# The first block of a time-mix and FFN kernel: order of the k and r chunks, three of r's chunks in three float32r passes, and weight splits moved to the second block

## The chip, the core and the metric

The kernel runs on one core of a Trainium2 chip. The time is device microseconds of one execution. Engines are named as in the profile: PE (TensorE, matrix products), DVE (VectorE), ACT (ScalarE), POOL (GpSimd) and SP (SyncE, which issues most DMAs).

## The reference

For x of shape (4, 1024, 512) in fp32, with xn the layernorm of x:

```python
xx = concat([xn[:, 1:2], xn[:, :-1]], axis=1) - xn
k  = (xn + xx * time_mix_k) @ Wk.T        # 704 channels
r  = (xn + xx * time_mix_r) @ Wr.T
state_t = state_{t-1} * exp(-exp(time_decay)) + relu(k_t)
mix = layernorm((state * r) @ Wv.T) * ln_gamma + ln_beta
D   = gelu(fp16(xn) @ W0.T + bias0).astype(fp16)   # 2048 hidden units
ffn = (D @ W1.T + bias1).astype(fp16)
out = x + mix + ffn
```

## The kernel before, in words

The 4 x 1024 tokens are worked in eight **blocks** of 512 tokens. In every block the FFN is a loop over 16 **chunks** of 128 hidden units: `up` (L860) makes the accumulator pd of a chunk from 8 matmuls, four with the high halves of w0 and four with fp16 low halves; the gelu (L874) and a cast (L877) on ACT make d from it; `down` (L886) adds the chunk to four accumulators pe with 8 matmuls. `up` runs two chunks ahead of `down`. The time mix of the same block is woven into these chunks by hand: `piece(n, ...)` gives FFN chunk n a group of matmuls, `put(n, ...)` gives it jobs for the other engines, and `behind_w1[n]` a job after all these. Each engine works through its instructions in the order in which the code records them.

**k and r.** The 704 channels are five chunks of 128 and a half chunk. A matrix product with a full chunk takes one of two forms:

- In block 0, plain fp32: `raw_k` (L634), `raw_r` (L648), 4 matmuls with the weights as loaded; `raw_halves` (L658) makes the half chunks of k and r in 32 matmuls of 64 rows.
- In later blocks, `three_pass` (L687): weights and inputs are split into float32r terms; pa takes 8 matmuls (L693), pb takes 4 (L444); ACT copies pa out with a scale (`a`, L705) and DVE adds pb (`y`, L706). `half_pass` (L716, L722) does the half chunks.

k goes through a relu and the scan over tokens (L585); r is multiplied into the state (`gated`, L602).

**Splits.** `split_kr` (L290) makes the three float32r terms of a weight chunk: on DVE `u` (L278), `d` (L287) and term 2 (L298), on ACT two copies (L296, L297); the terms are stored to DRAM, and `load_kr` (L327) fetches them in later blocks. `split_x` does the like for inputs (L278, L338, L340, and L336 on ACT). `split_wv` (L309 on) splits the output weights; its half chunk, `split_wv(5)`, takes two operations on DVE (vu, vd) and four copies of 64 rows on ACT (L324, L325). `split` (L198 to L200) makes the high half of w0 or w1 on ACT and the low half on DVE; `load_w1` calls it in block 0 at the end of a chunk's jobs for the w1 of two chunks on, and `down` begins with the low half there.

**The next block's inputs.** During a block its successor's x is loaded, its statistics taken (L357), normalized (L361) and transposed in 16 `turn`s (L383), and mixed.

**Accumulators.** pd, pk, pr, pa, pb, ph, po, oa and ob share four PSUM banks of the pool `ps_mm` (`bank`). A bank can be written again when its reader is done: ACT for pd (gelu) and pa (`a`), DVE for pb (`y`). In blocks from 1 on the gelu of chunk n + 2 is recorded at the end of chunk n's jobs when n is odd, and after the next chunk's first steps when n is even.

**Before the FFN** block 0 makes k0, k1, k2 (L444, in pieces as the inputs come) and r0, r1, r2, and splits the first groups of w0 and w1.

Of the kernel before, what the change touches and what calls it, by code (L numbers as in the profile page):

```python
# [22 lines left out]
def time_mix_and_gelu_ffn(  # L23
# [40 lines left out]
    Q = 32  # L64
    QS = 62
    RAW_OUT = 1
    WV_FIRST = {0: 12, 1: 13, 2: 15, 3: 15, 5: 15}
    S = 4096.0
    WS = 4096.0
    MASK = -4096  # L70
# [57 lines left out]
    def load_raw(kind, h):  # L128
        w = part(f"w{'kr'[kind]}_{h}", F32)
        raw_w[kind, h] = w.rearrange("p (c k) -> p c k", c=NC)  # L130
        src = sources[kind].rearrange("(c p) k -> p c k", p=P)
        nc.sync.dma_start(raw_w[kind, h], src[:, :, h * P : (h + 1) * P])
# [32 lines left out]
    with tc.manual_schedule(engines={nc.sync.engine, nc.scalar.engine}):  # L165
        x_now = load_x(
            0,
            "x",
            (
                lambda: None,  # L170
                load_mix_rows,
                lambda: [load_raw(0, h) for h in range(FIRST)],
                load_late_rows,
            ),
        )
        for h in range(FIRST):
            load_raw(1, h)
    raw_half = part("raw_half", F32).rearrange("p (two c k) -> p two c k", two=2, c=NC)
    gamma_sb = const.tile([P, C], F32, name="gamma_sb")
    beta_sb = const.tile([P, C], F32, name="beta_sb")  # L180
# [27 lines left out]
    def load_w0(g, c, **home):  # L208
        w0_raw[c, g] = raw = part(f"w0raw_{g}_{c}", F32, **home)
        nc.sync.dma_start(raw, w0T[c * P : (c + 1) * P, g * TB : (g + 1) * TB])  # L210
# [21 lines left out]
        for n in range(NN)  # L232
    ]
    w1_raw = {}
    stores, late_stores = [], []

    def store_weights():
        while stores:
# [34 lines left out]
    half_w = [part(f"half_w_{kind}", tag="half", bufs=2) for kind in range(2)]  # L273
    half_w = [w.rearrange("p (c two k) -> p c two k", c=NC, two=2) for w in half_w]

    def truncated(raw, name, home=None):
        u = (home or temp)(name)
        nc.vector.tensor_scalar(u.bitcast(I32), raw.bitcast(I32), MASK, None, ALU.bitwise_and)  # L278
        return u

    begun = {}

    def begin_kr(kind, h, home):
        raw = raw_w[kind, h].rearrange("p c k -> p (c k)")
        u = truncated(raw, f"wu_{kind}_{h}", home)
        d = home(f"wd_{kind}_{h}")
        nc.vector.tensor_sub(d, raw, u)  # L287
        return u, d

    def split_kr(block, kind, h, **home):  # L290
        made.add((kind, h))
        name = f"{kind}_{h}"
        u, d = begun.pop((kind, h), None) or begin_kr(kind, h, temp)
        home = home or dict(tag="kr", bufs=6)
        terms = [part(f"wt_{name}_{p}", **home) for p in range(3)]
        nc.scalar.copy(terms[0], u)  # L296
        nc.scalar.activation(terms[1], d, AF.Copy, scale=S)  # L297
        nc.vector.scalar_tensor_tensor(terms[2], d, -S, u, ALU.mult, ALU.add)  # L298
        later = late_stores if (kind, h) == (1, NF - 1) else stores
        for p in range(3):  # L300
            later.append((kr_dram[kind, h][p].bitcast(F32), terms[p].bitcast(F32)))
        return [t.rearrange("p (c k) -> p c k", c=NC) for t in terms]

    def split_half():
# [123 lines left out]

    def split_xk(i, c):
        xks[i, c] = yield from split_x(xks[i, c], f"k_{i}_{c}")  # L430

    def split_xr(i, c):
        xrs[i, c] = yield from split_x(xrs[i, c], f"r_{i}_{c}")
# [251 lines left out]
        return after  # L685

    def three_pass(j, kind, h):  # L687
        xs = xks if kind == 0 else xrs
        w = ks.pop((j, kind, h))
        pa, pb = bank(f"pa_{j}_{kind}_{h}"), bank(f"pb_{j}_{kind}_{h}")  # L690
        for c in range(NC):
            for p in range(2):
                nc.tensor.matmul(  # L693
                    pa,
                    w[p][:, c, :],
                    xs[j, c][p],
                    start=(c == 0 and p == 0),
                    stop=(c == NC - 1 and p == 1),
                )
        for c in range(NC):  # L700
            product(pb, w[2], xs[j, c][2], c)

        def after():
            a, y = temp(f"a_{j}_{kind}_{h}"), temp(f"y_{j}_{kind}_{h}")
            nc.scalar.activation(a, pa, AF.Copy, scale=1.0 + 1.0 / S)  # L705
            nc.vector.scalar_tensor_tensor(y, pb, -1.0 / S, a, ALU.mult, ALU.add)  # L706
            if kind == 0:
                nc.scalar.activation(y, y, AF.Relu)  # L708
                yield
                scanned(j, h, P, state_tile(j, h), y)  # L710
            else:
                yield from gated(j, h, y)

        return after
# [194 lines left out]
    with tc.manual_schedule(engines={nc.sync.engine}):  # L909
        for c in range(NC):  # L910
            load_w0(0, c)
        for n in range(AHEAD + 2):
            load_w1_raw(n)
        for h in range(FIRST, NF):
            load_raw(0, h)
            load_raw(1, h)
        for kind, src in enumerate(sources):
            nc.sync.dma_start(
                raw_half[:, kind], src.rearrange("(c p) k -> p c k", p=P)[:, :, H0:]
            )  # L920
        for c in range(NC):
            load_w0(1, c)
        x_next = load_x(1, "x")
        for c in range(NC):
            load_w0(2, c)
# [4 lines left out]

    engines = {e.engine for e in (nc.tensor, nc.vector, nc.scalar, nc.sync)}
    with tc.manual_schedule(engines=engines):
        for kind in range(2):
            begun[kind, 0] = begin_kr(kind, 0, lambda name: part(name, F32))
        first_x16(0)
        for h in range(FIRST):
            finished(raw_k(0, h, pks[h])())
        for c in range(1, NC):
            first_x16(c)
        xf = ffn_input(0)  # L940
        finished(raw_r(0, 0)())
        several(split_w0, (0, 0), (0, 1))
        finished(raw_r(0, 1)())
        several(split_w0, (0, 2), (0, 3))
        w1s = [load_w1(0, n) for n in range(AHEAD)]
        gated_last = raw_r(0, 2)
        several(split_w0, (1, 0), (1, 1))
        several(split_kr, (1, 0, 0), (1, 1, 0))
        finished(gated_last())
        waiting = []  # L950
        for n in range(AHEAD):
            products, gelu = up(0, n)
            several(products, *[(p,) for p in HIGH_FIRST])
            waiting.append((gelu(), w1s[n]))
            split_w0(1, 2 + n)
        store_weights()
# [4 lines left out]
    with tc.manual_schedule(engines=engines):  # L961
        for i in range(len(blocks)):
# [3 lines left out]
            pieces, bg, early = defaultdict(list), defaultdict(list), defaultdict(list)  # L966
            behind_w1 = defaultdict(list)

            def put(n, fn, *args):
                bg[n].append(lambda: fn(*args))  # L970

            def fetch_kr(block, kind, h):
                if (kind, h) not in made:
# [25 lines left out]

            if i == 0:  # L1000
                state["x"] = x_next
                piece(1, raw_k, i, 3)
                piece(3, raw_r, i, 3)
                piece(5, raw_k, i, 4)
                piece(7, raw_r, i, 4)
                piece(9, raw_halves, i)
                for c in range(NC):
                    put(2 + c - (c == 0), split_w0, 2, c)
                    put(c // 2, load_w0, 3, c)
                    put(5 + c, split_w0, 3, c)  # L1010
                put(1, stats, *range(NS))
                put(3, lambda: norm_apply(j, state["x"]))
                for n, *which in (
                    (0, 1, 2), (1, 0, 1), (1, 1, 3), (3, 0, 2), (5, 0, 3), (7, 0, 4), (7, 1, 1)
                ):
                    if which in ([1, 2], [1, 3]):
                        behind_w1[n].append(lambda w=which: split_kr(1, *w, **OWN))
                    else:
                        put(n, split_kr, 1, *which)
                put(4, turn, 0, 1)  # L1020
                put(5, turn, 1, 5)
                put(7, turn, 5, 10)
                put(8, turn, 10, 11)
                put(9, turn, 11, 16)
                put(9, load_late_constants)
                put(12, split_half)
                for g in range(NN // G):
# [3 lines left out]
            else:  # L1031
                order = [(0, h) for h in range(NF)] + [(1, h) for h in range(NF)]
                halves_ahead_of = (3 if i == LAST else NF, NF)
                for k, (kind, h) in enumerate(order):
                    for half in range(2):
                        if k == halves_ahead_of[half]:
                            piece(half_at[half], half_pass, i, half)
                    piece(full_at[k], three_pass, i, kind, h)
                    if (kind, h) not in made:
                        put(1, fetch_kr, i, kind, h)  # L1040
                    elif k > 1:
                        put(full_at[k - 2], fetch_kr, i, kind, h)
                xr_at = {1: (2, 3, 4, 5), LAST: (1, 2, 2, 3)}.get(i, (2, 2, 3, 3))
# [15 lines left out]
            if j <= LAST:  # L1059
                for c in range(NC):  # L1060
                    put((10, 10, 11, 12)[c], x16, j, c)
                for c, n in enumerate(mix_at):
                    early[n].append((j, c))
                    put(n, mixed, j, c)
                    put(n + (n == 10), split_xk, j, c)
                for h, n in {0: WV_FIRST, 1: {NF - 1: 2}}.get(i, {}).items():
                    put(n, split_wv, h)
                put(13, fetch_kr, j, 0, 0)
                put(14, fetch_kr, j, 0, 1)

            pe = [ps_e.tile([P, C], F32, tag="pe", name=f"pe_{i}_{s}") for s in range(NS)]
            for n in range(NN):
# [68 lines left out]
                    behind_works.append(lambda gelu=gelu, w1=w1: (gelu(), w1))  # L1141
                elif paired:
                    waiting.append((gelu(), w1))
                if (i, n) == (1, 6):
                    stores.extend(late_stores)
                store_weights()
            if not tail:
                e16s = [rounded(i, s, pe[s]) for s in range(NS)]
# [64 lines left out]
```

## Time and profile before

| what | us |
| --- | --- |
| median of 3 runs | 853.61 (853.30 to 853.65) |
| profiled execution | 853.32 |
| its span | 851.5 |
| PE busy | 847.1 |
| DVE busy | 678.1 |
| ACT busy | 434.0 |
| PE in block 0 from 40.80 to 130.40 | 89.51 of 89.60 |
| PE in block 1, 130.40 to 233.70 | 103.30 of 103.30 |

The page of the profile first gives the busy time of each engine, then the span in 40 slices with busy tenths in each. The chain of waits, further down, is followed back from the last instruction to what released each step: a row is its start in us, its duration, engine, tile and source line. A timeline lists one engine's instructions in order: start, duration, engine, line, operation, the tile written and the tiles read, their shapes; in brackets stands the idle time ahead of it and what ended it.

The raw chunks ahead of the FFN and in it, the FFN's pd and pe and the three-pass chunks all lie on PE, one after the other; the jobs for DVE and ACT lie beside them.

### The profile page before, as it was taken

Reading aid. Unit: us, or ns where it says so; the run is one execution under the profiler, and the core shown is the slowest. Engines: PE = TensorE matmul, PEld = TensorE weight load, DVE = VectorE, ACT = ScalarE, POOL = GpSimd, SP = SyncE. Lnnn points to the kernel's source line nnn. Section 1 sums busy time; section 2 is a strip of 40 time slices with the busy share of each in tenths; the row PEclk is TensorE's granted clock in tenths of the full one; section 3 lists DMA queues with packets and bytes.
Section 4 is the critical chain, followed back from the end, with each engine's and each line's share of the span. In section 5 each row is a group of like instructions: output and inputs, shape, how many; then the busy total and the mean of one; then the engine's idle time right before and its main releaser. Section 6 shows DMA issues by size and latency. Waiting matters only on the chain.

```text
span 851.5 us, 11300 instructions
## 1 busy us (share of the span) xinstructions
PE 847.1 (99%) x3756; PEld 592.4 (70%) x3756; DVE 678.1 (80%) x1114; ACT 434.0 (51%) x740; POOL 77.5 (9%) x145
## 2 busy tenths in 40 slices
PE   9999999999999999999999999999999999999998
PEld 8555546776766777766767767767767667776776
DVE  7689898898868978689786888779796897876446
ACT  5866764556444572544634456344653545534422
POOL 1100000000121002000021001100011200200002
PEclk9999999999999999999999999999999999999999
DMA  9976976753485635846458455494455755467513
GB/s 291 342 250 239 297 212 224 229 189 124 149 283 174 210 121 159 288 154 194 161 168 283 146 167 180 160 304 146 154 184 171 267 169 184 125 222 248 168 55 112
DMA packets 121766, 168.30 MB, mean 198 GB/s; under 512 B 21583, under 2 KB 57836, under 8 KB 121708
## 3 DMA queue, kind: packets, MB, share of 16 engines
q1 hardware_dynamic: 121260, 166.91, 60.7%
q8 instruction: 30, 0.49, 0.2%
q10 hardware_dynamic: 448, 0.66, 0.2%
q14 instruction: 28, 0.23, 0.1%
HBM read 142.88 MB, written 24.64 MB: 197 GB/s over the span
## 4 chain that ended last, share of the span: by engine, by line
PE 95%; DVE 3%; ACT 1%; issue 0%; DMA 0%; ACTq 0%
PE pd L860 26%; PE pe L886 26%; PE pa L693 15%; PE oa L790 7%; PE pb L444 7%; PE ob L798 4%; PE ph L722 3%; PE po L749 2%; PE pr L444 2%; PE ob L800 1%; PE pk L444 1%; PE pkr L667 0%; DVE stx L357 0%; DVE wd L287 0%; DMA x<-in_L_attn_x 0%
## 5 line engine op out<-in xcount | busy, mean ns | idle before, releaser
L886 PE MATMUL pe<-w,d 128*128 128x512 f32 (+1 forms) x1008 | 262.0, 388 | 0.1
L860 PE MATMUL pd<-xf,w0h 128*128 128x512 f32 x512 | 151.7, 418 | 0.0
L860 PE MATMUL pd<-x,w0l 128*128 128x512 f16 x512 | 132.2, 381 | 0.0
L874 ACT ACTIVATE d<-pd,late_sb 128x512 f16<-128x512 f32 x128 | 87.1, 681 | 81.5 <-PE pe L886 51.8
L860 PEld LDWEIGHTS pd<-xf,w0h 128*128 128x128 f32 x512 | 96.1, 188 | 29.0 <-issue 4.3
L886 PEld LDWEIGHTS pe<-w,d 128*128 128x128 f32 x504 | 94.7, 188 | 22.1
L706 DVE SCALAR_TENSOR_TENSOR y<-pb,a 128x512 f32<-128x512 f32 x70 | 48.2, 689 | 65.6 <-PE pb L444 55.3
L886 PEld LDWEIGHTS <-d 128*128 128x128 f16 x524 | 50.6, 98 | 60.4 <-issue 1.2
L860 PEld LDWEIGHTS <-w0l 128*128 128x128 f16 x512 | 44.1, 98 | 62.4 <-issue 17.4
L877 ACT CAST d<-d 128x512 fp32r<-128x512 f16 x128 | 79.4, 620 | 10.3 <-PE pe L886 6.3
L383 DVE STREAM_TRANSPOSE xnT<-x 32x512 f32<-32x512 f32 x112 | 78.7, 702 | 2.2
L705 ACT ACTIVATE a<-pa 128x512 f32<-128x512 f32 x70 | 41.8, 597 | 72.5 <-PE pa L693 72.3
L351 POOL TENSOR_SCALAR ry<-mvy 128x1 f32<-128x1 f32 x32 | 18.8, 589 | 421.2 <-DVE mvy L358 421.2
L693 PE MATMUL pa<-hk,kr 128*128 128x512 f32 x140 | 54.5, 389 | 0.0
L693 PE MATMUL pa<-lk,kr 128*128 128x512 f32 x140 | 54.5, 389 | 0.0
L790 PE MATMUL oa<-wv,hg 128*128 128x512 f32 x140 | 54.5, 389 | 0.0
L790 PE MATMUL oa<-wv,lg 128*128 128x512 f32 x140 | 54.5, 389 | 0.0
L693 PE MATMUL pa<-hr,kr 128*128 128x512 f32 x136 | 52.9, 389 | 0.0
L693 PE MATMUL pa<-lr,kr 128*128 128x512 f32 x136 | 52.9, 389 | 0.0
L708 ACT ACTIVATE y<-y 128x512 f32<-128x512 f32 x35 | 22.1, 631 | 52.7 <-DVE y L706 52.7
L805 DVE SCALAR_TENSOR_TENSOR oy<-ob,oa 128x512 f32<-128x512 f32 x28 | 19.3, 689 | 26.2 <-PE ob L800 26.2
L336 ACT CAST hg<-ug 128x512 fp32r<-128x512 f32 x35 | 21.7, 620 | 34.6 <-DVE ug L278 34.5
(167 smaller groups left out, 1387.1 us busy)
## 6 DMA issues: line engine op xcount, KB each, us to landing
kr<-krd SPq DMA_DIRECT2D x207, 256.0 KB, 4.3
w<-w1d SPq DMA_DIRECT2D x112, 256.0 KB, 2.7
w<-w1d SPq DMA_DIRECT2D x112, 128.0 KB, 2.7
w0l<-w0d SPq DMA_DIRECT2D x108, 128.0 KB, 3.5
xres<-in_L_attn_x SPq DMA_DIRECT2D x32, 256.0 KB, 4.7
x<-in_L_attn_x SPq DMA_DIRECT2D x31, 256.0 KB, 4.9
krd<-wt SPq DMA_DIRECT2D x30, 256.0 KB, 2.3
out<-xres SPq DMA_DIRECT2D x28, 256.0 KB, 3.5
```

The lines of the kernel that those rows point to most:

```text
L383: nc.vector.transpose(dst[i * Q : (i + 1) * Q, :, :, j, :], src[j * Q : (j + 1) * Q, :, :, i, :],)
L444: return nc.tensor.matmul(dst, w[:, c, :], src, start=(c == 0), stop=(c == NC - 1))
L693: nc.tensor.matmul(pa, w[p][:, c, :], xs[j, c][p], start=(c == 0 and p == 0), stop=(c == NC - 1 and p == 1),)
L705: nc.scalar.activation(a, pa, AF.Copy, scale=1.0 + 1.0 / S)
L706: nc.vector.scalar_tensor_tensor(y, pb, -1.0 / S, a, ALU.mult, ALU.add)
L722: nc.tensor.matmul(pa, w[:, c].rearrange("p two k -> p (two k)"), xs[j, c][p], start=(c == 0 and p == 0), stop=(c == NC - 1 and p == 1),)
L790: nc.tensor.matmul(pa, gs[i, h][p][:, cols], wv[h][p], start=(h == 0 and p == 0), stop=(h == NF - 1 and p == 1),)
L798: nc.tensor.matmul(pb, gs[i, h][2][:, cols], wv[h][2], start=(h == 0), stop=False)
L860: nc.tensor.matmul(pd, weights(c, p), src[c][p], start=(c == 0 and p == order[0]), stop=(c == NC - 1 and p == order[1]),)
L874: nc.scalar.activation(d16, pd, AF.Gelu, bias=b0_sb[:, n : n + 1], scale=1.0 / WS)
L877: nc.scalar.copy(d, d16)
L886: nc.tensor.matmul((sums or pe)[s], d[p][:, s * P : (s + 1) * P], w1[p][:, cols], start=(n == first and p == order[0]), stop=(n == end(s) ...
```

## The change

Block 0 and block 1 are reordered; blocks 2 to 7 keep their code.

- Ahead of the FFN, all five full chunks of k (raw) and r0, instead of k0 to k2 and r0 to r2. The begun splits there (r's and k's chunk 0) and `split_kr(1, 0, 0)`, `split_kr(1, 1, 0)` are taken out.
- In block 0's FFN: the half chunks at chunk 1 (were at 9), raw r4 at chunk 3, and r1, r2, r3 by `three_pass` at chunks 5, 7, 9 (raw k3, r3, k4, r4 stood at 1, 3, 5, 7). The r inputs are split for this (`split_first_xr`, three at chunk 0, one at chunk 1) and r's weight chunks 1 to 3 at chunks 3, 5, 7.
- k's chunks 0, 1 and 2 are split at chunks 10, 11 and behind w1 at 5. The splits of k's chunks 3 and 4 and of r's chunks 0 and 4 move to block 1, at its FFN chunks 1, 2, 4, 6 (before, one split of a chunk stood there, r's chunk 4, at chunk 1). These four are used in block 1 as they are made.
- `split_wv(5)` moves from block 0's chunk 15 to block 1's chunk 3, `split_wv(4)` in block 1 from chunk 2 to 8.
- The turns at chunks 7, 8, 9 become 5 to 11, 11 to 12, 12 to 16. The raw weights are loaded in another order. The late stores of r's chunk 4 go with the others.

```diff
-    WV_FIRST = {0: 12, 1: 13, 2: 15, 3: 15, 5: 15}
+    WV_FIRST = {0: 12, 1: 13, 2: 15, 3: 15}
...
-        for h in range(FIRST):
-            load_raw(1, h)
+        for which in ((0, 3), (0, 4), (1, 0)):
+            load_raw(*which)
...
+    first_xr = {}
+
+    def split_first_xr(c):
+        first_xr[0, c] = yield from split_x(xrs[0, c], f"r_0_{c}")
...
     def three_pass(j, kind, h):
-        xs = xks if kind == 0 else xrs
+        xs = xks if kind == 0 else xrs if j > 0 else first_xr
...
-        for h in range(FIRST, NF):
-            load_raw(0, h)
-            load_raw(1, h)
         for kind, src in enumerate(sources):
             nc.sync.dma_start(
                 raw_half[:, kind], src.rearrange("(c p) k -> p c k", p=P)[:, :, H0:]
             )
+        for h in (4, 1):
+            load_raw(1, h)
         for c in range(NC):
             load_w0(1, c)
+        for h in (2, 3):
+            load_raw(1, h)
...
-        for kind in range(2):
-            begun[kind, 0] = begin_kr(kind, 0, lambda name: part(name, F32))
...
-        finished(raw_r(0, 0)())
+        finished(raw_k(0, 3)())
         several(split_w0, (0, 0), (0, 1))
-        finished(raw_r(0, 1)())
+        scanned_last = raw_k(0, 4)
         several(split_w0, (0, 2), (0, 3))
+        finished(scanned_last())
         w1s = [load_w1(0, n) for n in range(AHEAD)]
-        gated_last = raw_r(0, 2)
+        gated_last = raw_r(0, 0)
         several(split_w0, (1, 0), (1, 1))
-        several(split_kr, (1, 0, 0), (1, 1, 0))
         finished(gated_last())
...
-                piece(1, raw_k, i, 3)
-                piece(3, raw_r, i, 3)
-                piece(5, raw_k, i, 4)
-                piece(7, raw_r, i, 4)
-                piece(9, raw_halves, i)
+                piece(1, raw_halves, i)
+                piece(3, raw_r, i, NF - 1)
+                for h in range(1, NF - 1):
+                    piece(2 * h + 3, three_pass, i, 1, h)
...
-                for n, *which in (
-                    (0, 1, 2), (1, 0, 1), (1, 1, 3), (3, 0, 2), (5, 0, 3), (7, 0, 4), (7, 1, 1)
-                ):
-                    if which in ([1, 2], [1, 3]):
-                        behind_w1[n].append(lambda w=which: split_kr(1, *w, **OWN))
-                    else:
-                        put(n, split_kr, 1, *which)
+                for c in range(NC):
+                    put(c // 3, split_first_xr, c)
+                for h in range(1, NF - 1):
+                    put(2 * h + 1, first_kr, h)
+                put(10, split_kr, 1, 0, 0, **OWN)
+                put(11, split_kr, 1, 0, 1, **OWN)
+                behind_w1[5].append(lambda: split_kr(1, 0, 2, **OWN))
                 put(4, turn, 0, 1)
                 put(5, turn, 1, 5)
-                put(7, turn, 5, 10)
-                put(8, turn, 10, 11)
-                put(9, turn, 11, 16)
+                put(7, turn, 5, 11)
+                put(8, turn, 11, 12)
+                put(9, turn, 12, 16)
...
                     if (kind, h) not in made:
-                        put(1, fetch_kr, i, kind, h)
+                        put({(0, 3): 1, (0, 4): 2, (1, 0): 4, (1, 4): 6}[kind, h], fetch_kr, i, kind, h)
...
-                for h, n in {0: WV_FIRST, 1: {NF - 1: 2}}.get(i, {}).items():
+                for h, n in {0: WV_FIRST, 1: {NF: 3, NF - 1: 8}}.get(i, {}).items():
                     put(n, split_wv, h)
...
-                if (i, n) == (1, 6):
-                    stores.extend(late_stores)
```

More of the change, by code (lines that the diff above doesn't have):

```diff
@@ L234, in time_mix_and_gelu_ffn @@
     w1_raw = {}
-    stores, late_stores = [], []
+    stores = []
     def store_weights():
@@ L274, in time_mix_and_gelu_ffn, with truncated, begin_kr @@
     half_w = [w.rearrange("p (c two k) -> p c two k", c=NC, two=2) for w in half_w]
-    def truncated(raw, name, home=None):
-        u = (home or temp)(name)
+    def truncated(raw, name):
+        u = temp(name)
         nc.vector.tensor_scalar(u.bitcast(I32), raw.bitcast(I32), MASK, None, ALU.bitwise_and)
         return u
-    begun = {}
-    def begin_kr(kind, h, home):
+    def begin_kr(kind, h):
         raw = raw_w[kind, h].rearrange("p c k -> p (c k)")
-        u = truncated(raw, f"wu_{kind}_{h}", home)
-        d = home(f"wd_{kind}_{h}")
+        u = truncated(raw, f"wu_{kind}_{h}")
+        d = temp(f"wd_{kind}_{h}")
         nc.vector.tensor_sub(d, raw, u)
@@ L292, in split_kr @@
         name = f"{kind}_{h}"
-        u, d = begun.pop((kind, h), None) or begin_kr(kind, h, temp)
+        u, d = begin_kr(kind, h)
         home = home or dict(tag="kr", bufs=6)
@@ L298, in split_kr @@
         nc.vector.scalar_tensor_tensor(terms[2], d, -S, u, ALU.mult, ALU.add)
-        later = late_stores if (kind, h) == (1, NF - 1) else stores
         for p in range(3):
-            later.append((kr_dram[kind, h][p].bitcast(F32), terms[p].bitcast(F32)))
+            stores.append((kr_dram[kind, h][p].bitcast(F32), terms[p].bitcast(F32)))
         return [t.rearrange("p (c k) -> p c k", c=NC) for t in terms]
@@ L967, in time_mix_and_gelu_ffn, with put, first_kr @@
             behind_w1 = defaultdict(list)
-            def put(n, fn, *args):
-                bg[n].append(lambda: fn(*args))
+            def put(n, fn, *args, **home):
+                bg[n].append(lambda: fn(*args, **home) if home else fn(*args))
+            def first_kr(h):
+                ks[0, 1, h] = split_kr(0, 1, h)
             def fetch_kr(block, kind, h):
```

## The prediction

> **What bounds the kernel now.** I read the page from the top: the busy shares, the row of 40 slices, the chain of waits, then the timelines of VectorE (DVE), ScalarE (ACT) and TensorE (PE) where the change edits them. The page:
>
> ```profile
> PE 847.1 (99%) x3756; PEld 592.4 (70%) x3756; DVE 678.1 (80%) x1114; ACT 434.0 (51%) x740; POOL 77.5 (9%) x145
> PE   9999999999999999999999999999999999999998
> DVE  7689898898868978689786888779796897876446
> ```
>
> PE is the bound: 847.1 of 851.5 us, at the full granted clock in every slice, so PE work removed is gained and each PE wait added is paid in full at the end. But DVE is at 0.8 to 0.9 in block 0 and block 1 (the first nine or ten slices), where the change adds to it. The windows by block say it closer: DVE was busy 77.90 of the 89.60 us from 40.80 to 130.40 (block 0) and 90.01 of the 103.30 us of block 1, against 83.48 in block 2. The chain of waits over the first 135 us:
>
> ```profile
> 54.92 0.69 DVE w0l L200
> 55.61 1.83 DVE x L361 x4
> ...
> 59.73 0.70 DVE w L200
> ...
> 60.47 1.94 PE pe L886 x8
> 62.41 3.44 PE pk L444 x8
> ...
> 73.01 3.44 PE pr L444 x8
> ...
> 83.75 3.59 PE pkr L667 x32
> ...
> 130.51 1.81 PE pa L693 x8
> 132.33 0.91 PE pb L444 x4
> ```
>
> Up to 60.4 the split of w1 by DVE (L200) ends the wait and PE follows; from 60.47 PE runs alone. A raw chunk (two rows above, 8 records) is 3.44 us, a chunk in three passes 1.81 + 0.91 = 2.72 (last two rows). How thin the margin is stands in DVE's timeline:
>
> ```profile
> 77.47 3.56 DVE L383 STREAM_TRANSPOSE xnT<-x 32x512 f32<-32x512 f32 x5
> 81.06 0.69 DVE L200 SCALAR_TENSOR_TENSOR w<-w1raw,w 128x512 f16<-128x512 f32 x1
> ```
>
> This is the low half of w1 for chunk 9; it ends at 81.75, and PE's down matmuls of chunk 9, which begin with that half, start at 81.80. PE came with no margin: whatever delays DVE here delays PE.
>
> **PE's own work.** r1, r2, r3 go from 3.44 to 2.72: 3 x 0.72 = **2.16 us less**. Raw k3, k4, r0, r4, the halves (3.59) and all else only change places. Ahead of the FFN k3, k4 stand where r1, r2 stood, same shapes and same count; I take the first FFN matmuls where they were.
>
> [...]
>
> **Block 0's DVE.** New: four splits of x_r (12 DVE operations, 7.2 us at the 0.6 of a neighbouring split's pitch), y's of three chunks (0.69 each). Gone from block 0: the splits of k's chunks 3 and 4, r's 0 and 4 (1.8 each: 0.45+0.72+0.61), and wv_5 from chunk 15. I laid the changed kernel's list of DVE instructions out with these durations. w1's low half starts at (before / after): w1_5 59.73 / 58.78, w1_6 62.72 / 61.78, w1_7 69.74 / 68.83, w1_8 72.07 / 74.14, w1_9 81.06 / 82.63. From w1_7 to w1_9 are 11.32 us before, 13.80 after: the split of k's chunk 2 behind w1 at chunk 5 (+1.8), one split fewer at chunk 7 (-1.8), a sixth turn (+0.72), and waits for ACT copies (0.56, 0.42, 1.08 against 0.41: +1.65); y and g stand for the scan. The sum is 2.4; the layout's 2.48 is used.
>
> PE after, from pe of chunk 5 at about 60.5: r1 in place of k4, r2 in place of r4, so that it wants pe of chunk 9 at 80.26 (81.80 less 2 x 0.72; its first pe, with no wait before it, is 0.16 shorter, and starts 0.03 later). The low half of w1_9 is ready at 83.37. **Stall 3.1 us.** Then r3 (2.72) stands for the halves (3.59 plus the slower pd after it), 1.0 less, so chunk 10's pe comes at 89.75 against 89.18. The later low halves come 1 to 4 us later than before but at least 1.3 us ahead of PE. So block 0 eats its whole gain: block 1 begins **0.55 late** (bounds: -0.9, were w1_9 on time for all but 1.6 us, to +1.2).
>
> **Block 1, three waits.** Before, PE had none here. An accumulator bank (four, L444 and L860 share them) is free again when ACT has read it. In the changed kernel's instruction list pa of k's chunk 4 waits for d16_5 (gelu of pd_5), pa of r's chunk 1 for d16_9, pa of r's chunk 2 for the copy `a` of r's chunk 1. Before, ACT had them early:
>
> ```profile
> 152.36 0.62 ACT L336 CAST hr<-ur 128x512 fp32r<-128x512 f32 x1 [0.44 <-DVE ur L278]
> 152.89 0.68 ACT L874 ACTIVATE d<-pd,late_sb 128x512 f16<-128x512 f32 x1
> ...
> 175.15 0.62 ACT L620 CAST gh<-gl 64x512 fp32r<-64x512 f32 x1 [0.82 <-DVE gl L619]
> 175.80 0.69 ACT L874 ACTIVATE d<-pd,late_sb 128x512 f16<-128x512 f32 x1
> ...
> 180.79 0.60 ACT L705 ACTIVATE a<-pa 128x512 f32<-128x512 f32 x1 [0.59 <-PE pa L693]
> ```
>
> and PE began those pa at 155.63, 178.94 and 186.97.
>
> 1. The four copies of wv_5 (L324, L325) now stand on ACT between hr and d16_5 at chunk 3. They wait for vu_5, which DVE reaches only after the pair of stats (before 153.70 to 155.39, after to 155.44) plus 0.42: 155.86. Four copies at 0.66 (before, at chunk 15: 125.56 to 128.26, 2.70): to 158.53. d16_5 to 159.20. pa, wanted at 155.63 + 0.55 = 156.2, starts at 159.25: **+3.05**. If the copies were hidden, 0; nothing hides them, since ACT's rows start in the order of its list.
> 2. Behind that, `a` of k's chunk 3 comes at 160.3, y at 160.4, and DVE has the splits of r's chunk 0 (chunk 4) and r's chunk 4 (chunk 6), 3.6 us, that it had not; it runs without idle time. y of the half pass starts at 179.63 (before 171.82), gl follows as before, the copy gh at 182.95, then d16_9, 183.60 to 184.29. pa is wanted at 178.94 + 3.6 = 182.55 and starts at 184.3: **+1.7**.
> 3. wv_4's split (DVE 1.8) with its ACT copy at 192.9 stands ahead of the copy `a` of r's chunk 1 (193.4 to 194.0), which before ran at 180.79. pa of r's chunk 2 is wanted at 186.97 + 5.4 = 192.35, starts 194.0: **+1.7**.
>
> After that splits (wv_4 was at chunk 2) are behind it, PE's shift gives DVE time, and the margins are 0.5 to 3 us; the three kr chunks that are split here are not loaded (9 DMAs of 256 KB fewer; the kr issues take 4.3 us to land, and no wait in block 1 was for one). Blocks 2 to 7 have the same work in the same order. Of the moved DMAs, SP's list has nine issues fewer; raw loads go earlier than the halves, and the first to be needed at chunk 1 are the halves, 40 us after the start. I find none that lands late and put 0 on it (bounds -0.2 to +1).
>
> **Sum.** +0.55 + 3.05 + 1.7 + 1.7 = **+7.0**; with rounding in the layout, 7.06. The profiled execution took 853.32 us (span 851.5), the median of the three runs is 853.61, so the sum goes on 853.32: **860.4 us**.
>
> **Rivals.**
> - *The gain stays.* DVE keeps w1_9 before 80.3 and ACT d16_5 before 156.2, and the 2.16 us of PE time is all that counts: 853.32 - 2.16 = **851.2**. For it: PE alone is on the chain from 60.47. Against: the zero margin at 81.8 with 2.5 us more of DVE ahead of it. It is decided by those two times. Chance 0.09.
> - *Block 0's stall alone.* vu_5 is early enough or pa does not wait for d16_5: +0.55, **853.9**, within 0.2% (1.7 us, about what a measurement of this kernel can tell from no change). For it: the times in block 1 are worked out over 100 us of DVE. Chance 0.09.
> - *Some of the three waits.* The first remains and the next two, each less than 2 us and hung on DVE's lag, are absorbed: +3.6, **856.9**. For it: their two prices are differences of long sums. Chance 0.20.
> - *More lag.* DVE does not catch up before the out stage, and a fourth wait of the same size (1.7 to 3) follows: **863**. Chance 0.10.
> - *The forecast*, 858 to 862.5: chance 0.52.
>
> Faster by over 0.2% is only the first rival: 0.09. Same: the second: 0.09. Slower: 0.82. The range takes the forecast, the third and part of the last: **855.3 to 863**.
>
> **What would show it.** In the changed profile: pr rows in float32r of 1.81 + 0.91 at chunks 5, 7, 9 (right on PE's 2.16); a DVE w1 low half on the chain near 83, before pe of chunk 9 (right on block 0); block 1's pa of k's chunk 4 waiting 3 us for ACT's d16, with four wv copies ahead of it; two later waits near 183 and 193; block 2 as long as before. I am wrong if PE shows no idle time at 80 to 84, or if the idle time in block 1 lies behind a DMA.

## The result, and the profile after

The changed kernel takes 861.66 us (median of 4 runs, 861.63 to 862.13), the kernel before 853.63 (4 runs, 853.30 to 853.98): a ratio of 1.0095, 95% interval 1.0078 to 1.0113. It is 8.0 us slower. The profiled execution took 861.63, its span is 859.8 us.

The page of the changed kernel, the rows that answer to those shown of before, and PE's granted clock:

```profile
PE 847.3 (99%) x3768; PEld 594.9 (69%) x3768; DVE 686.3 (80%) x1129; ACT 436.9 (51%) x747; POOL 79.8 (9%) x145
...
PE   9998999899999999999999999999999999999998
...
DVE  6788898799877988789886897868796897876446
...
PEclk9999999999999999999999999999999999999999
```

PE was busy for as long as before (847.3 against 847.1), though it has less to do; the span is 8.3 longer, so PE now waits. Two slices of PE, the fourth and the eighth, stand at 8. Its waits, added up by what ended them (line, releaser, us in all, times, longest):

```profile
PE pa L695 <- ACT d L876: 3.6, 2, 2.2
PE pe L888 <- DVE w L200: 3.0, 1, 3.0
PE pa L695 <- ACT a L707: 1.4, 1, 1.4
```

Before, none of these three groups existed. In PE's timeline the four waits lie one after the other (the idle time stands in brackets):

```profile
83.55 3.45 PE L888 MATMUL pe<-w,d 128*128 128x512 f16 x8 [2.95 <-DVE w L200]
...
160.04 0.50 PE L695 MATMUL pa<-hk,wt 128*128 128x512 f32 x1 [2.24 <-ACT d L876]
...
185.12 0.50 PE L695 MATMUL pa<-hr,kr 128*128 128x512 f32 x1 [1.35 <-ACT d L876]
...
194.83 0.50 PE L695 MATMUL pa<-hr,kr 128*128 128x512 f32 x1 [1.38 <-ACT a L707]
```

The first row has something that a wait does not explain: eight pe matmuls took 3.45 us, against 1.94 before. The windows of the changed kernel around it tell why (stretch, its length, busy times of PE, PEld, DVE, ACT, POOL; then the granted clock, DMA share, GB/s):

```profile
78.00:80.60 2.60, 2.60 (x12) 1.49 (x11) 2.54 (x4) 2.57 (x6) 0.00 (x0) 1.00 0.79 295
80.60:83.50 2.90, 0.00 (x1) 0.00 (x0) 2.83 (x6) 2.28 (x5) 0.00 (x0) 0.97 0.26 98
83.50:85.00 1.50, 1.45 (x5) 0.61 (x4) 1.47 (x3) 0.00 (x0) 0.00 (x0) 0.50 0.26 87
85.00:86.00 1.00, 1.00 (x3) 0.78 (x3) 0.97 (x2) 0.00 (x0) 0.00 (x0) 0.50 0.96 178
86.00:87.00 1.00, 1.00 (x4) 0.79 (x3) 0.94 (x3) 0.00 (x0) 0.00 (x0) 0.63 0.88 336
87.00:88.00 1.00, 1.00 (x7) 0.80 (x6) 0.99 (x2) 0.63 (x1) 0.00 (x0) 1.00 0.26 91
```

PE stood still from 80.6 to 83.5, and at about 83.3 its clock fell to half, until about 86.7. What it did until then took about twice as long.

How far PE is behind the kernel before, at the points which the prediction named (start of the first matmul, from the timelines; forecast as summed there):

| PE starts | before | after | later by | forecast |
| --- | --- | --- | --- | --- |
| first pd | 29.61 | 29.70 | 0.09 | 0 |
| pe of chunk 9 | 81.80 | 83.55 | 1.75 | 1.57 |
| pe of chunk 10 | 89.18 | 91.35 | 2.17 | 0.57 |
| block 1, pa of k's chunk 0 | 130.35 | 132.52 | 2.17 | 0.55 |
| block 1, pa of k's chunk 4 | 155.47 | 160.04 | 4.57 | 3.6 |
| block 1, pa of r's chunk 1 | 178.78 | 185.12 | 6.34 | 5.3 |
| block 1, pa of r's chunk 2 | 186.80 | 194.83 | 8.03 | 7.0 |
| profiled execution | 853.32 | 861.63 | 8.31 | 7.06 |

From block 2 on nothing is added that matters (8.03 to 8.31).

### The profile page after: what moved, and what is told of

Read it like the earlier page. It is cut to its first block, busy times and chain, and to the rows that moved or that the text cites. A ratio compares the mean times of both kernels' runs of the same rounds, so it can differ in the third digit from the quotient of the medians.

```text
span 859.8 us, 11343 instructions
## 1 busy us (share of the span) xinstructions
PE 847.3 (99%) x3768; PEld 594.9 (69%) x3768; DVE 686.3 (80%) x1129; ACT 436.9 (51%) x747; POOL 79.8 (9%) x145
## 4 chain that ended last, share of the span: by engine, by line
PE 77%; DVE 3%; ACT 0%; issue 0%; DVEq 0%
PE pd L862 21%; PE pe L888 21%; PE pa L695 13%; PE oa L792 7%; PE pb L446 7%; PE ob L800 4%; PE ph L724 3%; PE ob L802 1%; DVE xnT L380 1%; DVE xres L841 0%; DVE x L358 0%; DVE e L835 0%; DVE y L708 0%; DVE mr L337 0%; DVE lr L335 0%
## 5 line engine op out<-in xcount | busy, mean ns | idle before, releaser
L708 DVE SCALAR_TENSOR_TENSOR y<-pb,a 128x512 f32<-128x512 f32 x73 | 50.2, 688 | 69.6 <-PE pb L446 54.9
L707 ACT ACTIVATE a<-pa 128x512 f32<-128x512 f32 x73 | 43.6, 598 | 72.9 <-PE pa L695 72.8
L695 PE MATMUL pa<-hk,kr 128*128 128x512 f32 x132 | 51.4, 389 | 0.0
L695 PE MATMUL pa<-lk,kr 128*128 128x512 f32 x132 | 51.4, 389 | 0.0
```

The lines of the kernel that those rows point to most:

```text
L695: nc.tensor.matmul(pa, w[p][:, c, :], xs[j, c][p], start=(c == 0 and p == 0), stop=(c == NC - 1 and p == 1),)
```

## The experiments

**The theory.** A single late instruction on DVE or ACT makes each of the four waits, by what stands ahead of it on its engine; and PE's wait of 2.95 us halved its clock besides. **Rivals.** DVE's added work as a whole comes out as waits wherever it is put; or the new rotation of the four banks makes them.

Medians below stand beside the kernel before on the same chip (853.45 to 853.66). In each profiled execution the first pd starts a little differently (29.46 to 31.07 us, also between kernels with the same code up to there), so differences of about 1 us between runs say little, and points of PE's timeline are given counted from it; "block 1" is its first pa, 100.74 in the kernel before and 102.82 in the changed one.

**1. The split of k's chunk 2 out of chunk 5.**

```diff
-                behind_w1[5].append(lambda: split_kr(1, 0, 2, **OWN))
+                behind_w1[12].append(lambda: split_kr(1, 0, 2, **OWN))
```

> The changed kernel with the split of k's chunk 2 behind w1 at chunk 12 instead of 5. My theory (DVE's load ahead of w1's low half for chunk 9 makes the wait in block 0, and that wait of 2.95 us also halves the clock for the next 3.3 us): the low half starts 1.8 us earlier, near 81.0 instead of 82.81; PE waits about 1.1 us there and keeps clock 1.0; block 1 starts about 3.3 us earlier than in the changed kernel. How much of it is kept depends on block 1: 858.3 us if its waits stay as they are, 860 if its first wait grows because DVE and ACT do not move with PE; I take 859.3. Rival (waits for ACT's copies, not the split, make w1 late): the low half moves by less than 0.7 us, the clock still falls, time about 861.5.

Measured: 861.22 us (860.48 to 861.57). The wait at chunk 9 is gone, the clock stays at 1.00 there, and PE comes to r3 at 52.52 from the first pd against 57.14: 4.6 us earlier, from moving 1.8 us of DVE. That is the cause of the first wait, and 4.6 is its price, with the clock, at this point of PE's list. But at chunk 13 the moved split stands ahead of the mixing, and ACT's copies xf come late; the clock falls there instead:

```profile
111.12 2.14 PE L862 MATMUL pd<-xf,w0h 128*128 128x512 f32 x4 [1.43 <-ACT xf L442]
```

```profile
112.00:113.00 1.00, 0.96 (x3) 0.37 (x2) 0.97 (x3) 1.00 (x3) 0.00 (x0) 0.98 0.95 242
113.00:113.40 0.40, 0.40 (x2) 0.17 (x2) 0.36 (x2) 0.40 (x2) 0.00 (x0) 0.50 1.00 379
```

(PE's timeline and the windows of this run; the clock is at 1.00 again from 116.4.) Block 1 starts at 102.28: nearly all is given back.

**2. The same split at chunk 9**, `behind_w1[9]`, where DVE had been idle for 1.53 us.

> The changed kernel with the split of k's chunk 2 behind w1 at chunk 9 instead of 5. With it at chunk 12 PE came to r3 4.6 us earlier (no wait at chunk 9, no fall of the clock), and lost that again at chunk 13, where the split stood ahead of the copies xf; at chunk 9 the profile of that run shows DVE idle for 1.53 us. My theory: the wait at chunk 9 is gone and nothing in block 0 takes its place, block 1 starts 4.6 us earlier, and the three waits of block 1 grow by what DVE and ACT cannot follow: 857.1 us if they follow wholly, 859.5 if by half. Rival (DVE's total in block 0 is too much wherever the split stands): a wait elsewhere in block 0, block 1 starts as in the changed kernel, 861.

Measured: 861.69 us (860.73 to 862.08). In block 0 two small waits remain (0.91 at chunk 12, 0.38 for xf) and block 1 starts at 100.78, level with the kernel before and 2.0 earlier than the changed one. The time does not move, a miss: the wait for d16_5 grows from 2.24 to 2.88 us and the clock now falls behind it, at 160.3 to 163.7. By the trace block 2 starts at 211.04 from the first pd against 212.05 in the changed kernel, so block 1 takes half of what PE gains in block 0; the other half is no more than the first pd differs between executions (30.89 here, 29.70 there).

**3. wv_5 behind the gelu of chunk 5.** Same work, other order on ACT.

```diff
-                for h, n in {0: WV_FIRST, 1: {NF: 3, NF - 1: 8}}.get(i, {}).items():
+                for h, n in {0: WV_FIRST, 1: {NF - 1: 8}}.get(i, {}).items():
...
                 elif paired:
                     waiting.append((gelu(), w1))
+                if (i, n) == (1, 3):
+                    split_wv(NF)
```

> The changed kernel with the split of wv_5 still at block 1's chunk 3, but recorded behind the gelu of chunk 5; same work, other order. My theory (the four wv_5 copies stand ahead of d16_5 on ACT; the second and third wait hang on the lag this gives DVE): the first wait (2.24 us and 0.3 of slower restart) goes and the two later ones (1.35 and 1.38) nearly go: 856.5 us. Rival A (DVE's added splits in block 1 are too much by themselves): only the first wait goes: 859.1. Rival B (the new rotation of the four accumulator banks makes PE wait, whatever the order on ACT): 861.7.

Measured: 860.55 us (860.43 to 860.82). The wait for d16_5 is gone (pa of k's chunk 4 starts 2.3 us earlier, counted from the first pd), with the bank rotation unchanged: rival B falls. The two later waits stay, and small new ones come in between (0.33 for the copy a of k's chunk 3, 0.45 for a cast of d). ACT and DVE of this run show why:

```profile
158.99 0.63 ACT L322 ACTIVATE wv<-vu 64x512 fp32r<-64x512 f32 x1
159.64 0.60 ACT L707 ACTIVATE a<-pa 128x512 f32<-128x512 f32 x1
```

```profile
160.27 0.69 DVE L708 SCALAR_TENSOR_TENSOR y<-pb,a 128x512 f32<-128x512 f32 x1 [2.60 <-ACT a L707]
```

The four copies still stand ahead of the copy a, and DVE stands idle for 2.60 us (3.84 in the changed kernel) waiting for it. I had put the later waits down to the first wait; the second comes from this idle time and from the splits that follow it. The third has its own copy ahead of it, as forecast. In the changed kernel's ACT timeline:

```profile
193.66 0.63 ACT L316 ACTIVATE wv<-vd 128x512 fp32r<-128x512 f32 x1
194.20 0.58 ACT L707 ACTIVATE a<-pa 128x512 f32<-128x512 f32 x1
```

**4. wv_5 back in block 0** (`5: 15` in `WV_FIRST` as before, not in block 1).

> The changed kernel with the split of wv_5 back at block 0's chunk 15. My theory: the first wait of block 1 goes and the others shrink, as with the order on ACT changed, and DVE has 1.1 us less to do in block 1: 856 us, unless block 0's last chunk now waits (then up to 858). Rival A (DVE's splits): 859. Rival B (banks): 861.7.

Measured: 857.75 us (857.47 to 857.93). The first and second wait of block 1 are gone, the third is left at 1.3 us, and the wait at chunk 9 with the fall of the clock is as in the changed kernel. One edit of place is worth 3.9 us.

**5. wv_4 back at block 1's chunk 2** (`{NF: 3, NF - 1: 2}`).

> The changed kernel with the split of wv_4 back at block 1's chunk 2. My theory (each of the three waits has its own blocking ACT or DVE work): the third wait goes (1.4 us and 0.3 of restart), but 1.8 us more of DVE stands ahead of vu_5 at chunk 3, so that d16_5 comes later by up to 1.8: about the same, 861.5 (860 to 862). Rival (wv_4 only matters where it stands ahead of the copy a at chunk 9): 860.0, first wait as it was.

Measured: 862.84 us (862.11 to 863.40). The second and third wait are gone, and the first has grown:

```profile
163.53 0.80 PE L695 MATMUL pa<-hk,wt 128*128 128x512 f32 x1 [4.48 <-ACT d L876]
```

(PE's timeline of this run.) Behind it the clock fell a second time, from 163.3 to 166.7, which I had not counted. The work moved ahead of d16_5, as the theory has it, but the price was higher.

**6. Both late wv splits later**, in block 1 at chunks 10 and 11 (`{NF: 10, NF - 1: 11}`).

> The changed kernel with both late splits of the output weights later in block 1: wv_5 at chunk 10 (was 3), wv_4 at chunk 11 (was 8); block 0 as changed. My theory (they stand ahead of what PE waits for): the first and third waits go, and the second shrinks, as ACT's four copies no longer hold back the copy a of k's chunk 3 and DVE has 1.1 us less: 856.2 us. Rival (the three kr splits alone put DVE so far behind that PE waits at chunks 8 and 9 anyway): 859.

Measured: 862.02 us (861.09 to 862.88), a miss. Nothing waits in block 1 up to r's chunk 3; against run 4, which has its third wait left with wv_4 at chunk 8, this shows wv_4's place as that wait's cause. Then r's chunk 4 waits (0.44) and the out stage (2.51 for d16 at its first oa), with a fall of the clock at 210.8 to 214.2.

**7. Both edits, 2 and 6.**

> The changed kernel with both edits: k's chunk 2 split behind w1 at chunk 9, wv_5 at chunk 10 and wv_4 at chunk 11 of block 1. My theory: no wait in block 0, at most a small one in block 1; the PE time saved by the three float32r chunks (2.16 us) then shows: 851.5 to 853 us, faster than before. Rival (the three kr splits of block 1 cost PE what they add to DVE, up to 3.6 us): 854 to 855.

Measured: 861.49 us (860.90 to 862.05), a plain miss. PE runs level with the kernel before as far as r's chunk 3 in block 1 (161.82 from the first pd, 161.73 before). Then r's chunk 4 and the out stage lose nearly 8 us: waits of 1.10, 2.47 and 0.58, and half clock from 208.8 to 215.7, two spells on end:

```profile
200.71 0.50 PE L695 MATMUL pa<-hr,wt 128*128 128x512 f32 x1 [1.10 <-ACT a L707]
208.04 0.50 PE L792 MATMUL oa<-wv,hg 128*128 128x512 f32 x1 [2.47 <-ACT d L876]
211.75 0.80 PE L792 MATMUL oa<-wv,hg 128*128 128x512 f32 x1 [0.58 <-ACT hg L333]
```

Chunks 10 and 11 have the next block's mixing and its splits, whose place the wv splits took: on ACT the copies of wv_5 now stand just ahead of the copy a at 200.06, those of wv_4 just ahead of d16 at 207.32. A split put off is late for somebody else. The half clock does not decide here: two of the four executions show a mean clock of 1.000, and they took 860.90 and 861.64 us, hardly less than the two with 0.996 (861.34, 862.05), though two spells are worth 3.4. They have no trace; what took that time in them is not shown.

**8. The kernel before, with DVE delayed ahead of w1's chunk 9.**

```diff
                 put(7, turn, 5, 10)
+                put(7, lambda: [turn(9, 10) for _ in range(5)])
```

> The kernel before, with five needless repeats of one turn at block 0's chunk 7 (each 0.72 us of DVE, same output), so that w1's low half for chunk 9 comes 3.6 us later and PE waits for it 3.5 us. My theory (a wait of PE of about 3 us also halves the granted clock for 3.4 us): the time grows by 3.5 and by about 1.6 more, less nothing, 858.7 us, with clock 0.5 for 3.4 us in the windows. Rival (the fall of the clock has to do with the changed kernel's matmuls, not with the wait): 857.1 us, clock 1.0.

Measured: 858.62 us (856.86 to 859.70). Its four executions, one kernel, took 856.86, 858.61, 858.64 and 859.70, with mean granted clocks of 1.000, 0.998, 0.998 and 0.996. The first is the profiled one: PE waited 3.67 us and the clock did not fall, which by itself is what the rival said.

```profile
85.35 1.94 PE L886 MATMUL pe<-w,d 128*128 128x512 f16 x8 [3.67 <-DVE w L200]
```

Eight pe took 1.94 as ever. So the wait costs itself (856.86 less 853.66 is 3.2, of a delay of 3.6). The other three executions took 1.75 or 2.8 more at a lower mean clock, though their code is the same; they have no trace, but 0.002 of 857 us is 1.7. The rival falls with run 12, whose trace has the fall in a kernel without any of the changed matmuls.

**9. r's chunks 1 to 3 raw in the changed kernel**, `raw_r` in place of `three_pass`, and no `split_first_xr`.

> The changed kernel with r's chunks 1 to 3 raw (3.44 us each) at the same places and no splits of x_r; the weight splits and their places as changed. PE has 2.16 us more to do, DVE in block 0 12 split operations and three y fewer (9.3 us). My theory (the end of block 1 is set by DVE's and ACT's own work in block 1, whatever PE gained or lost before it): no wait in block 0, block 1 starts as in the kernel before, and its first wait grows to 3 to 3.7 us with the two others after it: 860.5 us, as slow as the changed kernel. Rival (what matters is DVE's total over blocks 0 and 1, which the x_r splits swell): the waits of block 1 go too: 853.6 to 855 us.

Measured: 860.71 us (860.41 to 861.41), as forecast. DVE has some 9 us less to do and PE 2.16 more, and the time moves by 1 us. Block 1 starts at 101.42; its waits are 2.33 with a fall of the clock behind, and 1.39 (0.9 in block 0). What sets block 1's end is mostly in block 1; neither the float32r chunks nor the x_r splits are the bulk of the loss.

**10. A version with the x_r splits on POOL**, and with k's chunks 3 and 4 split in block 0.

```diff
+        nc.vector.tensor_scalar(u.bitcast(I32), raw.bitcast(I32), MASK, None, ALU.bitwise_and)
+        nc.scalar.copy(h, u)
+        nc.gpsimd.tensor_sub(l, raw, u)
...
+        nc.gpsimd.tensor_scalar(t, l.bitcast(F32), -S, None, ALU.mult)
+        nc.gpsimd.tensor_tensor(m, t, u, ALU.add)
...
+                put(0, split_kr, 1, 0, 3)
+                put(1, split_kr, 1, 0, 4)
```

> A version drawn from the runs so far: of each x_r split only the first operation stays on DVE, the rest (subtraction, scaling, addition) goes to POOL; k's chunks 3 and 4 are split in block 0's chunks 0 and 1 and reloaded in block 1, k's chunk 2 behind w1 at chunk 9, wv_5 at block 0's chunk 15 and wv_4 at block 1's chunk 2 as in the kernel before. The three float32r passes of r1 to r3 stay. DVE in block 1 has then only one split more than before. My theory: no wait in block 0, at most 1 to 2 us of waits in block 1, the saved 2.16 us of PE show in part: 852 to 853.5 us. Rival (the x_r splits on POOL come late for chunk 5, or slow DVE beside them): a wait at chunk 5 and 855 us or more.

Measured: 863.90 us (861.96 to 864.15), a miss: PE waited 5.18 us for the low half of w1 at chunk 3 and had half clock for two spells. Counted from the first pd that half begins 5.3 us later than in the changed kernel, and 4.1 of these are there when DVE comes to the low half of w0 ahead of it. ACT's and DVE's timelines of this run:

```profile
47.46 0.63 ACT L199 ACTIVATE w0h<-w0raw 128x512 fp32r<-128x512 f32 x1 [3.61 <-POOL mr L441]
```

```profile
48.13 1.08 DVE L200 SCALAR_TENSOR_TENSOR w0l<-w0raw,w0h 128x512 f16<-128x512 f32 x1 [3.42 <-ACT w0h L199]
```

ACT's copy w0h waited for POOL, whose operations take 1.26 to 2.15 us where DVE's took 0.69, and DVE waited for that copy; the added split of k's chunk 4 lies behind it. (Why this copy waits for POOL's mr is not shown.) Beside POOL's rows two of DVE's took 1.79 and 1.76 us. POOL's and DVE's timelines:

```profile
39.53 1.57 POOL L440 TENSOR_SCALAR tr<-lr 128x512 f32<-128x512 f32 x1
42.43 1.73 POOL L437 TENSOR_TENSOR lr<-xr,ur 128x512 fp32r<-128x512 f32 x1
```

```profile
40.51 0.69 DVE L285 TENSOR_TENSOR wd<-wk,wu 128x512 f32<-128x512 f32 x1
41.24 1.79 DVE L296 SCALAR_TENSOR_TENSOR wt<-wd,wu 128x512 fp32r<-128x512 f32 x1
42.95 1.76 DVE L200 SCALAR_TENSOR_TENSOR w<-w1raw,w 128x512 f16<-128x512 f32 x1
```

A low half of w1 took 1.76 instead of 0.69 us, but DVE stood idle for longer than that right behind it, so this row did not make the wait. In block 1, though, no wait is left, with two kr splits fewer there, wv_5 in block 0 and wv_4 at chunk 2.

**11. Four edits of place.**

```diff
-                behind_w1[5].append(lambda: split_kr(1, 0, 2, **OWN))
+                behind_w1[9].append(lambda: split_kr(1, 0, 2, **OWN))
...
-    WV_FIRST = {0: 12, 1: 13, 2: 15, 3: 15}
+    WV_FIRST = {0: 12, 1: 13, 2: 15, 3: 15, 5: 15}
...
-{(0, 3): 1, (0, 4): 2, (1, 0): 4, (1, 4): 6}
+{(0, 3): 1, (0, 4): 2, (1, 0): 4, (1, 4): 9}
...
-{NF: 3, NF - 1: 8}
+{NF - 1: 10}
```

> The changed kernel with four edits of place: k's chunk 2 split behind w1 at chunk 9, wv_5 at block 0's chunk 15, and in block 1 r's chunk 4 split at chunk 9 (was 6) and wv_4 at chunk 10 (was 8). The x_r splits and the three float32r chunks stay. My theory (each wait is made by what stands ahead of the late ACT instruction, and block 0 keeps about no gain): block 1 starts within 0.5 us of the kernel before, the first wait is gone, the second goes, the third becomes at most 1.5 us: 854.5 us (853 to 856). Rival (DVE's added work of blocks 0 and 1, some 9 us, comes out as PE waits wherever it is put): 858 or more.

Measured: 856.69 us (856.34 to 857.72, 7 runs), ratio to before 1.0030 (1.0019 to 1.0042), clock 1.00 throughout. All three waits at pa are gone, the one at chunk 9 and the fall of the clock too, and five of the eight us with them, by order alone. What is left in the profiled execution, the slowest (857.72): 0.91 at chunk 12, 0.35 for xf, 1.31 in the out stage, and 1.2 where pe of block 1's first chunk waits in small pieces for DVE to read out block 0's accumulators. Block 1 starts at 101.90 and block 2 at 206.84 from the first pd, 2.9 later than before (203.94). The first pd itself starts 1.46 later here (31.07): k0's first 18 matmuls took 3.46 us against 2.25. The 2.16 us of PE time are saved and do not show.

**12. The kernel before with wv_5 alone moved.**

```diff
-    WV_FIRST = {0: 12, 1: 13, 2: 15, 3: 15, 5: 15}
+    WV_FIRST = {0: 12, 1: 13, 2: 15, 3: 15}
...
-                for h, n in {0: WV_FIRST, 1: {NF - 1: 2}}.get(i, {}).items():
+                for h, n in {0: WV_FIRST, 1: {NF: 3, NF - 1: 2}}.get(i, {}).items():
```

> The kernel before with one edit: wv_5 split at block 1's chunk 3 instead of block 0's chunk 15; DVE and ACT do no more than before. My theory (order on ACT: the four copies stand ahead of d16_5): PE waits at pa of k's chunk 4 by 3.5 us, the clock may fall behind it (1.6 us), and no wait follows at chunks 8 and 9, as DVE has not the added splits: 857.3 us, or 858.9 with the fall of the clock. Rival (only DVE's added work makes these waits): 853.6 us.

Measured: 858.77 us (858.63 to 860.01). In a kernel without any of the added DVE work the wait is there:

```profile
157.85 0.63 ACT L325 ACTIVATE wv<-vu 64x512 fp32r<-64x512 f32 x1
158.50 0.69 ACT L874 ACTIVATE d<-pd,late_sb 128x512 f16<-128x512 f32 x1
```

```profile
159.24 0.80 PE L693 MATMUL pa<-hk,kr 128*128 128x512 f32 x1 [3.39 <-ACT d L874]
```

(ACT's and PE's timelines.) 3.39 us, half clock about it from 158.4 to 165.2, and no wait at chunks 8 and 9: d16_9 is ready 3.1 us before PE comes for it. Order on ACT makes the first wait; the second needs the added splits as well. (The third hangs on wv_4, which stays at chunk 2 here.)

## Why the prediction was right, and where it was short

- **"PE work removed is gained and each PE wait added is paid in full":** the second half holds as a sum. The four waits (7.92) and the clock (1.71), less the 2.16 saved, make 7.5 of the 8.3; the rest is about what a start behind a wait costs over the idle time (2.40, 1.77 and 1.69 by the table for 2.24, 1.35 and 1.38). It is no price list: run 2 takes most of the first wait away and run 9 does PE's 2.16 again without the x_r splits, and the time moves by 0 and by 1 us less, since block 1's first wait then grows or draws the fall of the clock. The first half never came to show: the forecast has block 0 eat the gain, but run 11, without the wait at chunk 9, does not show it either.
- **PE's own gain, 2.16:** right and invisible. PE wanted pe of chunk 9 at 80.6 (forecast 80.26; its own terms give 80.23).
- **Block 0's stall:** the low half of w1_9 began at 82.81, forecast 82.63; the wait was 2.95, forecast 3.1. The step that failed is the next sentence, "Then r3 (2.72) stands for the halves ... so chunk 10's pe comes at 89.75": it came at 91.35. The term "stall" was mis-sized: it costs its 2.95 us and 1.6 for the clock behind it. Run 12 shows that the fall comes with waiting (3.39 us there) and not with the change, and run 8 that a wait of 3.67 us can go without it.
- **First wait in block 1:** shown (runs 3 and 12). The size, 2.40 against 3.05, is short by about as much as PE came late from the clock, partly made up by d16_5 at 159.30 instead of 158.53.
- **Second and third wait:** 1.77 and 1.69 by the table, forecast 1.7 and 1.7. But "Behind that" was only half the cause: run 3 took the first wait away and left these; for the second it is ACT's copies ahead of the copy a, and the splits, that set DVE back: run 4 (the splits without the copies) and run 12 (the copies without the splits) have no second wait. The third is wv_4's split, as forecast (runs 4 and 6).
- **DMAs at 0:** right; no PE wait of the changed kernel ends at a DMA. (Runs 1 to 3, the same ahead of the FFN, waited 0.3 to 0.5 us for wk there.)
- **The rivals.** The gain (851.2) was decided by w1_9 before 80.3 and d16_5 before 156.2; they were ready at 83.5 and 160.0. "Block 0's stall alone" fell with d16_5 too. "More lag" named a fourth wait of 1.7 to 3 us: a cost of its size came (1.7), as a slow clock and not as a wait.
- **What the range rests on.** 861.66 lies 1.3 above the forecast, and that is partly luck: block 0's step came out 1.6 too small, and the first wait of block 1 0.65 too large, in part because PE came late. The layout by rows held to 0.2 us over 50 us of DVE's work in block 0 and to about 1 us at d16_9 (184.38 against 183.60).

**What stays open.** Run 11 still has PE waiting in four places; whether DVE's and ACT's work in blocks 0 and 1 leaves an order without waits is not shown. Which waits halve the clock is known only in part (below).

## What to carry to other kernels

When the bound engine has no idle time, a saving on it is kept only if the engines that feed it can come earlier too: here 2.16 us of matmul time were saved, and the first late instruction on DVE or ACT cost more. Before moving a job, find the instruction behind it on its engine for which the bound engine waits (a low half, a gelu that frees a bank, a copy), and read how long before it is due it is ready now; that margin, not the engine's busy share, is the price list. A wait of the bound matmul engine can cost more than its length, here 1.7 us of clock beside a wait of 2.95: look at the granted clock just after it, and in more than one execution, for one kernel can differ there (mean clocks of 1.000, 0.998, 0.998 and 0.996 in run 8).

## What the runs showed of the hardware

**The clock fell in portions of one size.** Summed over windows of 2 us from 40 to 226, the clock lost (its missing share times the time) is 1.70 to 1.72 us in the changed kernel and in runs 1, 2, 3, 4 and 9, 3.40 to 3.42 in runs 5, 6, 7, 10 and 12, and nothing in the kernel before and in the profiled executions of runs 8 and 11: at half clock, one spell of 3.4 us or two. In run 5 it fell at about 84.8 and again at about 163.3, in run 6 at about 84.5 and 210.8; in runs 7, 10 and 12 the two spells lie on end (6.8 us from about 208.8, 54.1 and 158.4).

**The length of a wait did not by itself decide the fall.** Waits of 2.92 to 2.95 us halved the clock in the changed kernel and in runs 3 to 6, and in run 1 it fell behind a wait of 1.43 us and four matmuls that took 2.14 us instead of 1.08, while 2.24 us in the changed kernel and 3.67 us in one execution of run 8 did not halve it. At the seven other falls (runs 2, 5, 6, 7, 9, 10 and 12) stand waits of 2.33 to 5.18 us. What made the difference is not shown.

The half clock stayed for a second 3.4 us in the three spells whose first 3.4 us held 0.58, 0.80 or 2.40 us of PE's waiting (runs 7, 12 and 10), and not in the ten with 0.3 or less.

**DVE was slow beside POOL in run 10.** The same 128x512 operations that take 0.69 us took 1.76 and 1.79 us while POOL worked on fp32 tiles of that size, and POOL's own took 1.26 to 2.15 us. One row of run 10 does not agree: wd kept its 0.69 us at 40.51 while POOL's row of 39.53 still ran (POOL's times are rough). What parts these rows is not shown.
